# Gathering whole rows, copying them out in slot order and loading them by parts; turning the router's logits on VectorE

## The chip, the cores and the metric

The kernel runs on one core of a Trainium2 chip. The core has a matrix engine (PE), a vector engine (DVE, VectorE), a scalar engine (ACT), a general engine (POOL, GpSimd) and SP, which here only issues DMAs. SP and ACT issue DMAs through hardware queues, POOL through a software queue; all of them end on the same 16 DMA engines. The metric is the device time of one execution in microseconds. Differences are stated against the kernel before.

## What is computed

x has 4 x 1024 tokens of 1024 numbers. The part of the reference that matters here, cut down:

```python
xn = layernorm(x)                       # per token
q, k, v = xn @ Wq.T + bq, xn @ Wk.T + bk, xn @ Wv.T + bv
kv_sum = cumsum((elu(k) + 1) * v, axis=tokens)      # per batch row
s = ((elu(q) + 1) * kv_sum * SCALE) @ Wo.T + bo
logits = xn @ router_w.T                # 8 experts, top 2, at most 256 tokens an expert
h = gelu(buf @ w1.T + b1) @ w2.T + b2   # same weights for every expert
g = silu(sum over the kept experts of probability * h)
out = x + s * g
```

All experts share w1 and w2, so a token needs its h once, and g is zero for a token that no expert kept. So out differs from x in at most 8 x 256 = 2048 tokens.

## The kernel before, in words

Every float32 number goes through PE as a rounded high part and a low part, and each product of two numbers as three matmuls. The work has two stages.

**Token blocks** (to 451 us). The first 2304 tokens go in blocks of 512 (four and a half). A block is normed row by row, its normed rows are stored in HBM (`xnd`), read back by quarters of 256 columns so that 32 x 32 transposes on VectorE turn them (`turned`, L249), and split into `xt`. For each of 8 chunks `kv_block` multiplies by a piece of Wk and one of Wv (L169, 24 matmuls a piece), forms the running sums and stores them in HBM (`kvs`). Side work (norms, transposes, routing, gathers) is laid out in a list of steps by `put`, and `step()` runs the next entry twice per chunk and part. The order on PE, DVE and ACT is written out by hand; on SP and POOL the framework orders the work of this stage, but for instructions marked `in_turn`, which keep program order. The last entry of a step list that concerns this change comes in the last block, which multiplies 512 and 256 tokens side by side and so has 32 steps.

*Router.* `router` (L333 to L355) multiplies each block by the router's weights (`rws`, high and low parts side by side in 16 columns) into `pl` (16 x 512), ACT copies it into `lt` (L344), and one step later `total` turns it on PE: per 128 tokens a matmul of `lt` as weights with `ssum` (L349) that also adds high and low parts; VectorE copies the result into `lg` (L350).

*Lists.* `routing` ranks the experts, finds each token's slot, and scatters token numbers and weights into `lst` in HBM, in slot order, by 18 indirect DMAs (L586). Slots 0 to 2047 are four `Slots` objects of 512. `places` reads the numbers four times over into `raw` and forms `at` = 4 x token + quarter (L617, L623); `load` reads numbers and weights (`it`, L629) and forms `eighth` and `half`.

*Gathers.* `quarters` (4 indirect DMAs for 128 tokens, rows of 1 KB) and `eighths` (4, rows of 512 B) bring rows by `at` and `eighth` straight into the layout that `turned` needs (all at L661). `chosen_items` fetches slots 0 to 1023 into `gx` in the last block, turns them into `work`, and `chosen_sums` forms what the first products need. The first quarters of w1 go into two tiles `raw[0]`, `raw[1]` by loads that are listed at the last block's first step (the framework issues them at 18 and 30 us).

**Products** (from 451 us). Two passes p = 0, 1 over 1024 slots each. A pass has 70 products of 48 matmuls (L1121): a 7-product recursive scheme stands for each 8 quarter products, as `features` (7 products; right operand b from the tokens) and `outputs` (7), for four parts of the hidden layer (w1, w2), then `queries` with Wq and `result` with Wo. Each product takes units a and b (2 + 2 tiles of 1 MB, high and low parts), in three buffers a side. In `features` of all parts but the very first, b is loaded ready-made from HBM (`b<-xtd`, L1091, 2 MB a product; the first part stores it there, L1235); in `result` from `wod`. Quarters of the weights come as `raw` (L834, L1184, 1 MB each). `wprep_items` and `xprep_items` prepare Wo's operands and the next pass's tokens (fetch, turn, split, store in `xtd`, L693) in small buffers (`s4`, eight). The order is written out by `on(n, phase, f)`: step n runs beside product n, in phases load, pre, cast0, evac, low0, add, cast1, mid, low1, post, raw. Here PE, DVE, ACT and SP, and the marked POOL instructions, keep program order.

In this stage `xprep_items` fetches rows for pass 1 by `quarters` (steps 13, 15, 28, 30, into `g`), and `queries` fetches sums by `eighths` (steps 42, 44, 50 and 57 of each pass, into `gk`, turned 2 or 3 steps later). Both are issued by POOL, which doesn't wait for PE and so runs ahead of the steps when buffers are free.

`ht` and `y0` are tiles of 128 x 2048 for one quarter of an operand or result, `raw` are five such.

Of the kernel before, what the change touches and what calls it, by code (L numbers as in the profile page):

```python
# [8 lines left out]
F32 = mybir.dt.float32  # L9
# [28 lines left out]
NC = NT // P  # L38
# [8 lines left out]
def tile_first_tokens(  # L47
# [42 lines left out]


# [15 lines left out]
    acol = cp.tile([P, 1], F32, name="acol")  # L107
    for a in range(NA):
        nc.gpsimd.memset(acol[a * SQ : (a + 1) * SQ], float(a))

    ssum = kp.tile([2 * NE, NE], F32, name="ssum")
    nc.gpsimd.tensor_tensor(
        ssum, ident[: 2 * NE, 0:NE], ident[: 2 * NE, NE : 2 * NE], ALU.add
    )
# [4 lines left out]
    lg = kp.tile([P, NE, NC], F32, name="lg")  # L119

    carry = kp.tile([P, 6 * DC], F32, name="carry")[:, :DC]
# [211 lines left out]
    def router(xt, b, j0, j1):  # L333
# [3 lines left out]
        for k in range(DC):  # L337
            for h in range(2):
                nc.tensor.matmul(  # L339
                    pl[: 2 * NE], rws[:, k], xt[:, h, k, cols],  # L340
                    start=k == 0 and h == 0, stop=k == DC - 1 and h == 1,
                )
        lt = tp.tile([2 * NE, BT], F32, tag="t512", bufs=5, name=f"lt_{b}_{j0}")
        nc.scalar.copy(lt[:, :w], pl[: 2 * NE])  # L344

        def total():
            pr = mmp.tile([P, NJ, NE], F32, tag="mm", name=f"pr_{b}_{j0}")
            for j in range(j1 - j0):
                nc.tensor.matmul(pr[:, j], lt[:, j * P : (j + 1) * P], ssum, start=True, stop=True)  # L349
            nc.vector.tensor_copy(  # L350
                lg[:, :, b * NJ + j0 : b * NJ + j1],
                pr[:, : j1 - j0].rearrange("p j e -> p e j"),
            )
# [247 lines left out]
    class Slots:  # L601


        def __init__(self, s):
# [3 lines left out]
            self.raw = cp.tile([P, NB, 1], I32, name=f"raw_{s}")  # L608
            self.at = cp.tile([P, NB, 1], I32, name=f"at_{s}")
            self.eighth = cp.tile([P, 2, NB], I32, name=f"eighth_{s}")  # L610

        def places(self):

            rows_ap = lst[self.s * BT : (self.s + 1) * BT, :]
            for a in range(NA):
                in_turn(
                    nc.gpsimd.dma_start(  # L617
                        part_of(self.raw, a),
                        rows_ap[:, 0:1].rearrange("(b j) w -> j b w", j=SQ),
                    )  # L620
                )
            in_turn(
                nc.gpsimd.tensor_scalar(self.at, self.raw, float(NA), acol, ALU.mult, ALU.add)  # L623
            )

        def load(self):
# [3 lines left out]
            for h in range(2):  # L630
                nc.gpsimd.tensor_scalar(
                    self.eighth[:, h], self.at[:, :, 0], 2.0, float(h), ALU.mult, ALU.add
                )
                nc.gpsimd.tensor_scalar(
# [6 lines left out]
        def quarters(self, g, src, j):  # L641

            for b in range(NA):
                gather(
                    g[:, b * FQ : (b + 1) * FQ],
                    src.rearrange("n (a f) -> (n a) f", a=NA),
                    self.at[:, j * NA + b],
                )

        def eighths(self, g, src, h, j):  # L650

            for b in range(NA):
                gather(
                    g[:, b * P : (b + 1) * P],
                    src.rearrange("n (a h f) -> (n a h) f", a=NA, h=2),
                    self.eighth[:, h, j * NA + b : j * NA + b + 1],
                )
# [11 lines left out]
    def xprep_items(p, buf):  # L669
# [3 lines left out]
        def item(j):  # L673
            g, v = {}, {}

            def fetch():
                for i in range(2):
                    g[i] = buf(f"g{p}_{j}_{i}")
                    slots[2 * p + i].quarters(g[i], xnd, j)
# [112 lines left out]
    rws = kp.tile([P, DC, 2 * NE], F32R, name="rws")  # L792
# [14 lines left out]

    def chosen_items():


        def item(i, j):
# [10 lines left out]
            slots[i].quarters(g, xnd, j)  # L822
# [809 lines left out]
```

## Time and profile before

| what | us |
| --- | --- |
| median of 17 runs | 2037.32 |
| lowest and highest of the runs | 2020.40, 2047.21 |
| the profiled execution's own time | 2019.86 |
| its span, first to last instruction | 2018.1 |
| DVE busy, ACT busy, POOL busy | 1509.7, 747.0, 418.5 |
| 36 matmuls pr (L349), busy | 4.8 |
| 192 gathers (L661), POOL busy | 151.5 + 45.5 + 33.8 |
| bytes moved by DMA | 400.17 MB, 198 GB/s |

A group in the profile names line, engine, operation, what it writes and reads, the count, busy time, mean ns of one, and the idle time just before with what ended it. A wait line names the engine and line that waited, who released it, the sum, the number of times and the longest. "issue" is a wait for nothing that the profile shows. A timeline line has start, length, engine, line, what and how many. A line of the table by stretches has the stretch, its length, the busy time (and number) of PE, of PE's weight loads, of DVE, ACT and POOL, then the granted clock of PE, the mean busy share of the 16 DMA engines, and GB/s.

### The profile page before, as it was taken

Reading aid. Unit: us, or ns where it says so; the run is one execution under the profiler, and the core shown is the slowest. Engines: PE = TensorE matmul, PEld = TensorE weight load, DVE = VectorE, ACT = ScalarE, POOL = GpSimd, SP = SyncE. Lnnn points to the kernel's source line nnn. Section 1 sums busy time; section 2 is a strip of 40 time slices with the busy share of each in tenths; the row PEclk is TensorE's granted clock in tenths of the full one; section 3 lists DMA queues with packets and bytes.
Section 4 is the critical chain, followed back from the end, with each engine's and each line's share of the span. In section 5 each row is a group of like instructions: output and inputs, shape, how many; then the busy total and the mean of one; then the engine's idle time right before and its main releaser. Section 6 shows DMA issues by size and latency. Waiting matters only on the chain.

```text
span 2018.1 us, 22522 instructions
## 1 busy us (share of the span) xinstructions
PE 1966.5 (97%) x8872; PEld 1621.7 (80%) x8872; DVE 1509.7 (75%) x1422; ACT 747.0 (37%) x876; POOL 418.5 (21%) x403
## 2 busy tenths in 40 slices
PE   8999999999999999999899999999999999999995
PEld 7877877888888788887588888888888888888884
DVE  7868876578897896895597786596586586697794
ACT  3323332225534543542342552342343342342460
POOL 2001103551033124118212016500000000303014
PEclk9999999999999999999899999999999999999998
DMA  8867857638359559547416579715614614715567
GB/s 313 242 194 241 266 143 158 208 121 305 117 200 354 208 195 369 227 147 269 178 48 213 175 260 321 275 42 173 243 42 169 248 42 168 270 45 196 188 205 152
DMA packets 121011, 400.17 MB, mean 198 GB/s; under 512 B 13792, under 2 KB 38368, under 8 KB 99168
## 3 DMA queue, kind: packets, MB, share of 16 engines
q1 hardware_dynamic: 79360, 320.95, 45.6%
q0 software_dynamic: 23104, 61.43, 10.1%
q10 hardware_dynamic: 18432, 16.26, 3.3%
q8 instruction: 72, 1.18, 0.2%
q14 instruction: 43, 0.35, 0.1%
HBM read 317.83 MB, written 88.10 MB: 201 GB/s over the span
## 4 chain that ended last, share of the span: by engine, by line
PE 81%; DVE 9%; DMA 3%; issue 3%; ACT 1%; POOL 1%; SPq 0%; ACTq 0%; DVEq 0%; POOLq 0%
PE ps L1121 63%; PE pk L169 9%; PE pv L169 9%; DMA b<-xtd 2%; DVE a L866 2%; DVE b L866 1%; DVE work L1048 1%; DVE hid L1048 1%; PE pl L339 1%; DVE raw L1045 1%; DVE wo L176 1%; DMA xtd<-o 1%; DVE hid L1045 0%; DMA wr_w<-in_wk 0%; POOL g L661 0%
## 5 line engine op out<-in xcount | busy, mean ns | idle before, releaser
L1121 PE MATMUL ps<-b,a 128*128 128x512 f32 x6720 | 1532.0, 390 | 14.3 <-issue 10.2
L1121 PEld LDWEIGHTS ps<-b,a 128*128 128x128 f32 x6720 | 1262.5, 188 | 283.4 <-issue 21.7
L863 ACT CAST a<-raw 128x1024 fp32r<-128x1024 f32 x140 | 147.1, 1052 | 457.8 <-PE ps L1121 323.0
L866 DVE TENSOR_TENSOR a<-raw,a 128x1024 fp32r<-128x1024 f32 x140 | 170.6, 1221 | 190.8 <-ACT a L863 172.0
L661 POOL DMA_INDIRECT gk<-kvs,eighth x128 | 151.5, 1184 | 605.1 <-DVE kv L249 567.0
L863 ACT CAST a<-hid 128x1024 fp32r<-128x1024 f32 x120 | 125.6, 1050 | 268.7 <-PE ps L1121 225.7
L169 PE MATMUL pk<-xt,ws_w 128*128 128x512 f32 (+1 forms) x792 | 183.1, 386 | 3.4 <-ACT xt L175 2.2
L169 PE MATMUL pv<-xt,ws_w 128*128 128x512 f32 (+1 forms) x792 | 181.8, 385 | 1.3 <-DVE ws_w L176 1.2
L866 DVE TENSOR_TENSOR a<-hid,a 128x1024 fp32r<-128x1024 f32 x120 | 146.2, 1220 | 41.1 <-ACT a L863 41.0
L169 PEld LDWEIGHTS pk<-xt,ws_w 128*128 128x128 f32 x792 | 145.1, 189 | 34.2 <-ACT xt L175 2.7
L169 PEld LDWEIGHTS pv<-xt,ws_w 128*128 128x128 f32 x792 | 145.2, 189 | 31.5 <-DVE ws_w L176 2.6
L1048 DVE TENSOR_TENSOR hid<-ps,hid 128x2048 f32<-128x2048 f32 (+1 forms) x69 | 125.1, 1821 | 57.7 <-PE ps L1121 35.9
L1045 DVE TENSOR_TENSOR raw<-raw,raw 128x2048 f32<-128x2048 f32 x62 | 141.9, 2288 | 0.8
L866 DVE TENSOR_TENSOR b<-raw,b 128x1024 fp32r<-128x1024 f32 x112 | 136.5, 1218 | 0.0
L863 ACT CAST b<-raw 128x1024 fp32r<-128x1024 f32 x112 | 117.3, 1047 | 0.0
L1048 DVE TENSOR_TENSOR work<-ps,work 128x2048 f32<-128x2048 f32 x40 | 91.4, 2286 | 29.2 <-PE ps L1121 29.2
L175 ACT CAST ws_w<-wr_w 128x1024 fp32r<-128x1024 f32 x64 | 66.1, 1049 | 85.8 <-issue 33.4
L1313 ACT ACTIVATE hid<-hid,bs 128x512 f32<-128x512 f32 x104 | 66.7, 713 | 57.4 <-DVE hid L1048 57.4
L176 DVE TENSOR_TENSOR ws_w<-wr_w,ws_w 128x1024 fp32r<-128x1024 f32 x64 | 77.7, 1214 | 10.0 <-ACT ws_w L175 8.7
L375 ACT ACTIVATE kb<-pk,bs 128x512 f32<-128x512 f32 (+1 forms) x40 | 25.9, 646 | 139.1 <-PE pk L169 95.2
L744 POOL DMA_DIRECT2D wod<-wo x28 | 20.2, 723 | 264.1 <-DVE wo L176 244.3
L214 POOL TENSOR_TENSOR r<-ve,mhalf 128x1 f32<-128x1 f32 x18 | 23.0, 1277 | 221.3 <-DVE ve L212 221.3
(183 smaller groups left out, 1292.8 us busy)
## 6 DMA issues: line engine op xcount, KB each, us to landing
b<-xtd SPq DMA_DIRECT2D x126, 1024.0 KB
raw<-in_w SPq DMA_DIRECT2D x64, 1024.0 KB
b<-wod SPq DMA_DIRECT2D x28, 1024.0 KB
wr_w<-in_wk SPq DMA_DIRECT2D x32, 512.0 KB
wr_w<-in_wv SPq DMA_DIRECT2D x32, 512.0 KB
xtd<-b SPq DMA_DIRECT2D x14, 1024.0 KB
wod<-wo POOLq DMA_DIRECT2D x28, 512.0 KB
xtd<-o POOLq DMA_DIRECT2D x28, 512.0 KB
```

The source lines that it names most:

```text
L169: nc.tensor.matmul(ps, ws[:, w, k], mv[:, x, k, c0:c1], start=n == 0, stop=n == len(order) - 1)
L175: nc.scalar.copy(dst[0], src)
L176: nc.vector.tensor_tensor(dst[1], src, dst[0].bitcast(F32), ALU.subtract)
L214: nc.gpsimd.tensor_tensor(r, ve, mhalf, ALU.pow)
L375: nc.scalar.activation(kb, ps, AF.Identity, bias=bcol)
L661: nc.gpsimd.indirect_dma_start(out=dst, out_offset=None, in_=src, in_offset=bass.IndirectOffsetOnAxis(ap=idx, axis=0),)
L863: nc.scalar.copy(self.parts[0], src)
L866: nc.vector.tensor_tensor(self.parts[1], self.src, self.parts[0].bitcast(F32), ALU.subtract)
L1045: nc.vector.tensor_tensor(dst, a, b, ALU.subtract)
L1048: nc.vector.tensor_tensor(dst, a, b, ALU.add)
L1121: nc.tensor.matmul(ps[m] if s["apart"] else ps[:, m], a(h, k, m), b(l, k), start=s["first"] and u == 0 and k == 0 and i == 0, stop=u == 1 ...
L1313: nc.scalar.activation(dst[:, m], src[:, m], AF.Gelu, bias=b1[:, fc : fc + 1])
```

## The change

Router: `rws` is widened to 32 columns, the last 16 zero; `pl` has 32 rows; the ACT copy, the matmuls with `ssum` and the tile `pr` go. `total` has VectorE turn `pl` by 32 x 32 blocks straight out of PSUM (four instructions a block of 512) and add high and low parts.

Gathers: `places`, `quarters` and `eighths` go, and with them `raw` (the list), `at`, `eighth`. For each 128 slots one indirect DMA brings whole rows (4 KB) into half of a tile that is free just then, and a plain DMA on POOL copies them into `xng` (tokens) or `kvg` (sums) in HBM, in slot order. `parts` then loads them by four plain DMAs on SP. Slots 0 to 1023 go through `ht`, `raw[0]` and `raw[1]` in the last block, all listed at its step 10 (six gathers, then copies out and gathers by turns); their loads and turns are listed at new steps, and the w1 quarters for `raw[0]` and `raw[1]` at step 22 in place of 0. Tokens of pass 1 go through `y0` at steps -1 to 7 of pass 0, sums of each pass through `ht` at steps 26 to 34. `fetch` in `queries` stands in the phase raw, that of `xprep_items` in the phase raw one step earlier. `lg` and `carry` get smaller tiles. The core of the diff:

```diff
@@ router
-                    pl[: 2 * NE], rws[:, k], xt[:, h, k, cols],
+                    pl[:SQ], rws[:, k], xt[:, h, k, cols],
...
-        lt = tp.tile([2 * NE, BT], F32, tag="t512", bufs=5, name=f"lt_{b}_{j0}")
-        nc.scalar.copy(lt[:, :w], pl[: 2 * NE])
         def total():
-            pr = mmp.tile([P, NJ, NE], F32, tag="mm", name=f"pr_{b}_{j0}")
-            for j in range(j1 - j0):
-                nc.tensor.matmul(pr[:, j], lt[:, j * P : (j + 1) * P], ssum, start=True, stop=True)
-            nc.vector.tensor_copy(
+            lt = tp.tile([P, BT], F32, tag="t512", bufs=5, name=f"lt_{b}_{j0}")
+            lt = lt[:, : (j1 - j0) * SQ].rearrange("p (j e) -> p j e", e=SQ)
+            for a in range(NA):
+                nc.vector.transpose(
+                    part_of(lt, a),
+                    pl[:SQ].rearrange("i (j a t) -> i a j t", a=NA, t=SQ)[:, a],
+                )
+            nc.vector.tensor_tensor(
...
@@ Slots
+        def gathered(self, dst, src, j, g):
+            r0 = self.s * BT + j * P
+            def rows_in():
+                gather(g, src, self.it[:, j, 0:1])
+            def rows_out():
+                in_turn(nc.gpsimd.dma_start(dst[r0 : r0 + P, :], g))
+            return rows_in, rows_out
+        def parts(self, g, src, j, c0=0, w=FQ):
+            nb = D // w
+            for a, rows_ap in enumerate(by_quarter(src, self.s * BT + j * P, nb, c0, w)):
+                nc.sync.dma_start(part_of(g, a).rearrange("p (b f) -> p b f", b=nb), rows_ap)
@@ last block
-                put([[lambda f=f: turns.append(f())] for f in chosen_items()], at=10 // half)
-                for at in (16, 18, 19, 20, 22, 23, 25, 26):
+                copies = [
+                    slots[j // NJ].gathered(xng, xnd, j % NJ, rows_of((ht, *raw)[j // 2 % 3], j))
+                    for j in range(2 * NJ)
+                ]
+                for k in range(2 * NJ + 6):
+                    if k >= 6:
+                        put([[copies[k - 6][1]]], at=10 // half)
+                    if k < 2 * NJ:
+                        put([[copies[k][0]]], at=10 // half)
+                for at, f in zip((14, 15, 16, 17, 19, 20, 21, 22), chosen_items()):
+                    put([[lambda f=f: turns.append(f())]], at=at // half)
+                for at in (18, 19, 20, 21, 23, 24, 25, 26):
                     put([[lambda: turns.pop(0)()]], at=at // half)
...
-                put([[lambda i=i: left_quarter(raw[i], w1, 0, i)] for i in range(2)])
+                put([[lambda i=i: left_quarter(raw[i], w1, 0, i) for i in range(2)]], at=22 // half)
@@ queries
-            for jj in range(4):
-                slots[2 * p + j].eighths(
-                    g[jj // 2][:, jj % 2 * BT : (jj % 2 + 1) * BT], kvs, i, jj
-                )
+            for half in range(2):
+                slots[2 * p + j].parts(g[half], kvg, 2 * half, i * P, P)
...
-            on(n0 + k, "load", lambda key=key: fetch(*key))
+            on(n0 + k, "raw", lambda key=key: fetch(*key))
@@ passes
+        for j in range(2 * NJ):
+            copies = [(26, slots[2 * p + j // NJ].gathered(kvg, kvs, j % NJ, rows_of(ht, j)))]
+            if p + 1 < NP:
+                sl = slots[2 * p + 2 + j // NJ]
+                copies.append((-1, sl.gathered(xng, xnd, j % NJ, rows_of(y0, j))))
+            for k, (rows_in, rows_out) in copies:
+                on(n0 + k + j, "post", rows_in)
+                on(n0 + k + j + 1, "load", rows_out)
...
-                    on(n0 + k + d, "post" if i else "load", f)
+                    on(n0 + k + d - (i == 0), "post" if i else "raw", f)
```

## The prediction

> **What bounds the kernel now.** I read the page's busy times first, then the timeline of PE, who made PE wait, the table by stretches of one product (10.9 us), and last the groups by line and the queues of POOL and SP.
>
> ```profile
> PE 1966.5 (97%) x8872; PEld 1621.7 (80%) x8872; DVE 1509.7 (75%) x1422; ACT 747.0 (37%) x876; POOL 418.5 (21%) x403
> PE ps L1121 <- issue: 10.2, 14, 1.6
> PE ps L1121 <- DMA b<-xtd: 4.0, 5, 1.1
> ```
>
> PE is busy for 97% of the span, so a change pays only where it takes matmuls off PE or takes away a place where PE runs below its pace. The pace: the chain of waits ends in one piece of 3072 matmuls (64 products of 48) in 696.62 us, 10.88 us a product. Places below it, in PE's timeline:
>
> ```profile
> 957.23 4.95 PE L1121 MATMUL ps<-b,a 128*128 128x512 f32 x20 [0.26 <-issue]
> 962.50 0.72 PE L1121 MATMUL ps<-b,a 128*128 128x512 f32 x2 [0.33 <-issue]
> 963.90 0.39 PE L1121 MATMUL ps<-b,a 128*128 128x512 f32 x1 [0.68 <-issue]
> ...
> 979.44 0.59 PE L1121 MATMUL ps<-b,a 128*128 128x512 f32 x1 [0.81 <-issue]
> 980.84 254.51 PE L1121 MATMUL ps<-b,a 128*128 128x512 f32 x1115 [0.81 <-issue]
> ```
>
> From 957 to 981 us PE issues one or two matmuls each 0.7 or 1.4 us, with nothing in the profile that it waits for ("issue"). From 913.14 to 1235.35 us are 1344 matmuls, 28 products: 322.2 us where 28 x 10.88 = 304.8 are due, so **17.5 us are lost**. There are two smaller places like it in the last token block: 331.01 to 354.24 us takes 23.2 us where two undisturbed weight pieces take 2 x 8.34 (6.6 lost), and 379.26 to 401.50 takes 22.2 where 2 x 8.34 are due (5.6 lost). Together 29.6 us. The busy sums hide part of it, since matmuls also last longer there; the granted clock (the first number after the five busy times) falls once PE idles:
>
> ```profile
> 335.00:350.00 15.00, 11.27 (x50) 8.29 (x49) 5.45 (x10) 2.02 (x2) 8.36 (x8) 0.89 0.90 141
> 385.00:393.00 8.00, 4.85 (x25) 4.18 (x24) 4.17 (x8) 2.21 (x4) 3.15 (x5) 0.83 0.85 258
> 955.00:982.00 27.00, 16.65 (x49) 10.00 (x48) 7.17 (x7) 3.08 (x3) 17.56 (x18) 0.73 0.52 183
> ```
>
> (us, then busy time and count of PE, PEld, DVE, ACT, POOL, then clock, DMA share, GB/s.) What the three have in common is POOL: it issues indirect DMAs back to back, one per 1.25 us, in all of them: the list scatters (320.8 to 346 us), the gathers gx (367 to 419) and 48 gathers gk (904.75 to 977). Against it: g (587 to 616, 751 to 779) and gk from 1050, 1252, 1713 and 1813 us come in such bursts too (that at 1252 of 36), and PE doesn't falter. So the burst may be needed, but it doesn't suffice.
>
> **The change, part by part.**
>
> *Router.* It removes 36 matmuls pr with their weight loads, and the ACT copy. The price is read from the timeline, as weight piece, pr, weight piece: 44.47 to 56.59 us is 12.12 us where two pieces take 10.88, so 1.24; the same at 109.61, 203.68 and 287.43; the half block (228.52 to 240.19) 0.79. Sum 4 x 1.24 + 0.79 = **5.75 us off PE**, which has no other work to put there. pl's weights grow from 16 to 32 columns: its 16 matmuls take 3.73 us, 0.233 each, and a full 128-column one 0.227, so nothing is added. VectorE gains four transposes of 32x128 and an add, and loses a 0.16 us copy. kr's transposes take 702 ns for 512 elements and 436 for 256: 1.04 ns an element and 170 fixed, so 0.30 each, 1.2 + 0.2 per block, some 6 us over five. DVE is at 0.7 to 0.85 here and weights are split three pieces (16 us) ahead of PE; the single PE wait on it was 1.2 us. Cost 0; without that cover 6. The zero columns of rws are one DVE instruction at the start, 0.2 us beside the first weight pieces. One bank of pl is held until the transposes, a step later; of four, two are enough for a chunk: 0.
>
> *Fewer, larger gathers.*
>
> ```profile
> L661 POOL DMA_INDIRECT gk<-kvs,eighth x128 | 151.5, 1184 | 605.1 <-DVE kv L249 567.0 <-issue 36.9 <-DMA gk<-kvs,eighth 0.9
> L661 POOL DMA_INDIRECT g<-xnd,at x32 | 45.5, 1422 | 9.8 <-issue 9.5 <-DMA g<-xnd,at 0.3
> L661 POOL DMA_INDIRECT gx<-xnd,at x32 | 33.8, 1055 | 18.7 <-issue 9.3 <-DVE work L249 9.2 <-DMA out<-in_x 0.3
> ```
>
> 192 gathers become 32 of 4 KB rows, each followed by a plain copy out: POOL goes from 231 us to about 32 x 1.2 + 32 x 0.8 = 64 us, worth nothing in itself (POOL is at 21%). What counts is that the long bursts are gone: six gathers in a row in the last block, then one per product. If bursts make PE falter, 5.6 (gx) and 17.5 (gk) go; the 18 scatters stay, and so do their 6.6. Bounds for this term: -29.6 (all three) to 0 (none); I take **-23.0**, by the bursts that the places lie in. The list loads for slots 0 and 1 shrink from eight of 2 KB to two of 4 KB, on POOL alone.
>
> [...]
>
> *More bytes.* 16.8 MB are now gathered, written and read again: +33.6 MB on 400. All of it has to fit beside PE's loads. The most that a 10.9 us stretch moved is 413 GB/s, 4.4 MB per product. In the first pass, products 29 to 36:
>
> ```profile
> 767.20:778.10 10.90, 10.90 (x50) 9.03 (x49) 4.07 (x5) 3.87 (x3) 7.41 (x8) 1.00 1.00 389
> 788.90:799.80 10.90, 10.90 (x50) 9.03 (x49) 7.19 (x10) 6.49 (x10) 2.58 (x3) 1.00 1.01 398
> 799.80:810.70 10.90, 10.90 (x50) 9.03 (x49) 7.00 (x8) 3.40 (x5) 2.54 (x3) 1.00 1.02 413
> 810.70:821.60 10.90, 10.90 (x50) 9.03 (x49) 8.86 (x9) 4.81 (x8) 2.57 (x3) 1.00 1.02 410
> ```
>
> The queues are full already: per product 2.1 MB of b, 1.05 of raw and 1.5 of xtd<-o are 4.6, and PE waits 0.8 us for b at 825. The copies of sums (steps 26 to 34) add 1.05 MB a product there: 1.05 x 4 = 4.2 MB over, 10 us at 0.41 MB/us. Most falls on POOL's own stores, since its chain of gather, copy, gather has one or two DMAs under way, while SP has several; late xtd<-o stores hold the small buffers that ACT writes (it waited 11.9 us for them before, with 0.8 reaching PE). Bounds 0 and 12; I take **+4**, nearer the row at 825. In the second pass the same steps stand at 290 GB/s (0.80); with 96 more they are just full: **+0.5**. The chosen rows' copies (steps -1 to 7, 451 to 530 us) meet 0.36 to 1.01; there b comes from SBUF and the raw loads have over a product of slack: 0. The gathers that POOL begins at 905 go away, and with them the wait of 0.89 us for b at 913: **-0.9**. (That of 0.27 at 1235 lies beside the accumulating stores, which stay.)
>
> [...]
>
> *Loads moved to SP.* 128 loads at 0.43 us (four xg take 1.74) are 56 us of a queue that waits 653 us for PE in the main part. They stand in SP's order before the next product's b loads, and a part load that had to wait would hold those. What it waits for: the copy out, 8 steps earlier for the sums and over 4 for the rows; and a small buffer: POOL's gathers found theirs at once except where POOL had run ahead of the transposes (waits of 72, 418 and 77 us); SP reaches it four steps after the transposes that free it. Behind them b's first half has 10.9 us until it is needed, and the 3.5 us of issue fit. In the last block the weights' loads are behind them: six gathers from about 360 us, copies out landed by 372 to 390 (an estimate: 1.25 us an issue, some 4 us a landing, like the 3.8 of kvs<-kr in the chain), turns due from 393 us on, and three split pieces (25 us) in hand. raw's w1 quarters move from 18 us to step 22 (about 410), needed at 444. Cost 0; if a load is late, DVE stands and PE after it.
>
> **Sum against the profiled execution:** -5.75 - 23.0 + 4.5 - 0.9 = -25.2; its time of 2019.86 us (span 2018.1) would be 1994.7. It is the fastest of those shown; their median is 2037.32, 17.5 above, and what fills that the profile can't show. I carry the difference over: 2037.3 - 25.2 = **2012 us**.
>
> **Rivals.**
> 1. *The faltering isn't the gathers'* (six bursts without it speak for this): -5.75 + 4.5 - 0.9 = -2.2, 2035 us, within the 0.3% (6 us) that a measurement can tell from no change. 0.13.
> 2. *Slower: the full queues become the bound* at products 29 to 36 of the first pass. PE bears the whole excess (12) and 2 in the second pass, and the faltering stays with the scatters, gathers and copies that remain: 12 + 2 - 5.75 = +8, 2046 us. It decides once the new waits for b and for xtd<-o's buffers pass 6 us more than the faltering that goes. For it: shares of 1.02 there; against: 0.8 us of wait so far. 0.23.
> 3. *Both:* the bursts' loss goes, but the queues take 14: -5.75 - 23.0 - 0.9 + 14 = -15.7, 2022 us. 0.08.
> 4. The forecast, 0.56; its own range is 1990 (all three places go, and some of the 17.5) to 2030.
>
> Faster 0.64, same 0.13, slower 0.23. The range runs from 1990 to 2046.
>
> **What would show it.** Right: no pr; PE's "issue" waits below 5 us and a granted clock of 1.00 at products 43 to 50; DMA at about 434 MB. Wrong: the same 0.7 us steps of PE at gathers or copies, b<-xtd waits above 8 us at products 29 to 36, ACT waiting for xtd<-o more than 20 us, or DVE waiting for gx, g or gk in the turns. If the median of the runs isn't moved by what the profile gains, my carrying over was wrong.

## The result and the profile after

The changed kernel takes 2058.46 us (median of 8 runs, 2054.13 to 2062.83), the kernel before 2035.98 beside it (47 runs, 2017.07 to 2048.35): ratio 1.0118, 95% interval 1.0091 to 1.0145. It is **slower by 22.5 us**, where 2012 was forecast, and lies above the forecast's range (1990 to 2046).

The busy times of the kernel after, and then who made PE wait (us in total, times, longest):

```profile
PE 1975.2 (96%) x8836; PEld 1621.4 (79%) x8836; DVE 1515.0 (74%) x1443; ACT 744.2 (36%) x871; POOL 230.7 (11%) x242
```

```profile
PE pv L163 <- DVE kb L413: 20.4, 1, 20.4
PE pk L163 <- ACT kb L374: 17.7, 1, 17.7
PE ps L1118 <- DMA b<-xtd: 13.9, 9, 3.1
```

The products' wait on "issue" (10.2 us before) is gone, as forecast, and POOL went from 418.5 to 230.7. New are two single waits of 38.1 us in the last token block. The wait for b grew from 4.0 to 13.9. PE's timeline and the table by stretches (columns as for before) show the two stalls and what they do to the clock; the last line is the stretch in which PE of the kernel before did only one or two matmuls at a time:

```profile
371.50 4.75 PE L163 MATMUL pk<-xh,ws_w 128*128 128x256 f32 x24 [17.69 <-ACT kb L374]
396.63 8.50 PE L163 MATMUL pv<-xt,ws_w 128*128 128x512 f32 x24 [20.38 <-DVE kb L413]
```

```profile
350.00:400.00 50.00, 11.93 (x46) 9.96 (x45) 5.98 (x11) 3.57 (x5) 15.79 (x25) 0.60 0.78 261
821.80:843.60 21.80, 19.86 (x88) 16.10 (x87) 16.98 (x18) 7.91 (x11) 6.29 (x8) 1.00 1.02 387
955.00:982.00 27.00, 25.34 (x112) 20.62 (x111) 19.67 (x13) 7.02 (x6) 1.28 (x2) 1.00 0.92 307
```

PE works 11.93 of 50 us from 350 on, at a granted clock of 0.60. Products begin at 492.65 and not at 451.54 us, 41.1 later; the spans of the two profiled executions differ by 39.3 (2057.4 against 2018.1). What stands behind the stalls is in the waits of SP and ACT, and in SP's timeline:

```profile
SPq L636 <- DMA xng<-ht: 53.6, 2, 45.7
ACT kb L374 <- DMA gx<-xng: 40.9, 1, 40.9
ACT ws_w L169 <- DMA gx<-xng: 24.5, 2, 21.3
DVE ws_w L170 <- ACT ws_w L169: 33.8, 11, 21.9
```

```profile
321.65 0.33 SPq L120 DMA_DIRECT2D wr_w<-in_wk  x1
367.78 11.41 SPq L636 DMA_DIRECT2D gx<-xng  x8
379.28 0.38 SPq L120 DMA_DIRECT2D wr_w<-in_wv  x1
386.71 5.38 SPq L636 DMA_DIRECT2D gx<-xng  x8
```

SP stands for 45.7 us at the first part load gx, until the copy out that it reads has landed, and no weight piece is loaded from 321.65 to 379.28 (before, six were, from 327.64 to 374.86). ACT's activation kb doesn't read gx; ACT waits for gx since a copy out<-in_x (L925) stands before it in ACT's order. In the program as built, the copies of ACT and the loads of SP are given the same eight completion semaphores by turns, and this copy waits for the one that the first gx load has to give back. The second stall comes the same way: PE waits for DVE (kb L413), DVE splits a weight piece before that and waits for ACT's half of the split (ws_w L169), and ACT waits behind its next copy for another gx load.

One more thing is in the timeline without a wait, the pace: one weight piece of 24 matmuls starts 5.60 us after the one before it, where it was 5.44, and a product takes 10.93 us in place of 10.89.

### The profile page after: what moved, and what is told of

Read it like the earlier page. It is cut to its first block, busy times and chain, and to the rows that moved or that the text cites. A ratio compares the mean times of both kernels' runs of the same rounds, so it can differ in the third digit from the quotient of the medians.

```text
span 2057.4 us, 22422 instructions
## 1 busy us (share of the span) xinstructions
PE 1975.2 (96%) x8836; PEld 1621.4 (79%) x8836; DVE 1515.0 (74%) x1443; ACT 744.2 (36%) x871; POOL 230.7 (11%) x242
## 2 busy tenths in 40 slices
DMA packets 149171, 433.69 MB, mean 211 GB/s; under 512 B 13280, under 2 KB 62432, under 8 KB 127328
## 4 chain that ended last, share of the span: by engine, by line
PE 82%; DMA 8%; DVE 5%; POOL 2%; issue 1%; ACT 1%; SPq 0%; ACTq 0%; DVEq 0%; POOLq 0%
PE ps L1118 66%; PE pv L163 8%; PE pk L163 8%; DMA b<-xtd 4%; POOL lst L585 1%; PE pl L333 1%; DMA xng<-ht 1%; DMA raw<-in_w 1%; DVE b L849 1%; DVE a L849 1%; DMA gk<-kvg 0%; DVE work L1045 0%; DMA xng<-raw 0%; DMA g<-xng 0%; DMA wr_w<-in_wk 0%
## 5 line engine op out<-in xcount | busy, mean ns | idle before, releaser
L1118 PE MATMUL ps<-b,a 128*128 128x512 f32 x6720 | 1533.9, 390 | 14.0 <-DMA b<-xtd 13.9
L163 PE MATMUL pv<-xt,ws_w 128*128 128x512 f32 (+1 forms) x792 | 187.6, 392 | 20.9 <-DVE kb L413 20.4
L163 PE MATMUL pk<-xt,ws_w 128*128 128x512 f32 (+1 forms) x792 | 188.0, 393 | 3.8 <-ACT xt L169 2.2
L163 PEld LDWEIGHTS pk<-xt,ws_w 128*128 128x128 f32 x792 | 146.2, 190 | 39.3 <-issue 2.9
L169 ACT CAST ws_w<-wr_w 128x1024 fp32r<-128x1024 f32 x64 | 66.1, 1046 | 101.4 <-issue 34.7
L1464 POOL DMA_INDIRECT out<-c,half x8 | 15.3, 1908 | 679.7 <-DVE c L1487 405.5
L376 DVE TENSOR_SCALAR ex<-kb 128x512 f32<-128x512 f32 (+1 forms) x40 | 15.8, 396 | 63.0 <-ACT kb L374 63.0
L640 POOL DMA_INDIRECT ht<-kvs,it x16 | 23.9, 1492 | 245.6 <-DVE a L849 240.9
```

Of the source, the lines that this page charges most:

```text
L163: nc.tensor.matmul(ps, ws[:, w, k], mv[:, x, k, c0:c1], start=n == 0, stop=n == len(order) - 1)
L169: nc.scalar.copy(dst[0], src)
L640: nc.gpsimd.indirect_dma_start(out=dst, out_offset=None, in_=src, in_offset=bass.IndirectOffsetOnAxis(ap=idx, axis=0),)
L1118: nc.tensor.matmul(ps[m] if s["apart"] else ps[:, m], a(h, k, m), b(l, k), start=s["first"] and u == 0 and k == 0 and i == 0, stop=u == 1 ...
```

## Experiments

The kernels of each section but the last ran on one chip, and ratios are to the kernel before on that chip, with 95% intervals. Differences in us are those of the medians; a ratio can differ from the ratio of the medians by some 0.002. The chips are of **two kinds**: on three the kernel before took 1992 to 1998 us, on three 2027 to 2049, much as in the first measurement (2036). Each chip was used in one session only, so what belongs to the chip and what to the session isn't told apart. Below, a chip "falters" where PE slows to single matmuls beside POOL's indirect DMAs, with "issue" as its wait. Kernels on different chips are compared through their ratios, or where the trace shows the place.

### Addresses, and the loads of the last block

The kernel before took 1992.13 us here.

*The kernel before, large tiles moved by 32 bytes:*

```diff
+    cp.tile([P, 8], F32, name="pad")
-    carry = kp.tile([P, 6 * DC], F32, name="carry")[:, :DC]
+    carry = kp.tile([P, 6 * DC + 8], F32, name="carry")[:, :DC]
```

> The kernel before with its large tiles moved by 32 bytes, nothing else, so that xt, work, hid, ht, raw, a2, b2 and y0 start at an address that is 0 mod 64, as they do in the changed kernel, in place of 32 mod 64. Theory A (the changed kernel's slower matmul pace, 0.2333 against 0.2267 us each in the token blocks and 10.93 against 10.89 us a product, comes from where its operands lie): the same two paces appear here, and the time grows by some 10 us in the token blocks and 6 in the products, 2036 to about 2052, ratio 1.008. Rival (the pace comes from the changed kernel's work, such as its wider router weights or its DMAs): paces 0.2267 and 10.89, time 2036, ratio 1.000.

Measured: 2008.63 us, 1.0076 (1.0062 to 1.0090), paces 5.60 and 10.93. Nothing but addresses was changed, so places of tiles cost 16 us (by the ratio 12 to 18). The rule "mod 64" fell later.

*The changed kernel with its tiles back in place* (the same two lines, `4 * DC + 8`):

> The changed kernel with the same 32 bytes put in, so that its large tiles start at 32 mod 64 as in the kernel before. Theory A: pace 0.2267 and 10.89 again, time 2058 less 16, about 2042, ratio 1.003; the two stalls of PE in the last token block (20.4 and 17.7 us) stay. Rival (the work, not the place): 2058, ratio 1.012.

Measured: 2049.78 us, 1.0294 (1.0280 to 1.0308), paces 5.44 and 10.89. The stalls stay, 26.7 and 21.2 us. The absolute numbers of the expectation were for the other kind of chip.

*The changed kernel with the loads gx and of w1's first quarters on POOL:*

```diff
-            slots[i].parts(g, xng, j)
+            slots[i].parts(
+                g, xng, j, issue=lambda *aps: in_turn(nc.gpsimd.dma_start(*aps))
+            )
...
-    [lambda i=i: left_quarter(raw[i], w1, 0, i) for i in range(2)]
+    [lambda i=i: left_quarter(raw[i], w1, 0, i, pool_dma) for i in range(2)]
```

> The changed kernel with two sets of loads of the last token block issued by POOL in place of SP: the 32 part loads gx and the two loads of w1's first quarters, both of which wait for copies out. Theory B (SP stands at the first gx load until its copy out has landed, the weights' loads behind it and, by a completion lane that a waiting gx load holds, ACT's copies of x too; so DVE and ACT stop and PE after them): both stalls go, 38 us and some 5 us of cold clock with them, 2058 to about 2015, ratio 0.990; products begin near 455 us and not at 493. Rival (the added 33.6 MB and the chain of gather, copy, load are themselves too slow, whoever issues): the turns still come late, the products begin 20 us or more late, the time stays above 2040, ratio over 1.002.

Measured: 2017.39 us, 1.0121 (1.0106 to 1.0137); products begin at 454.14, one stall of 11.5 us is left.

*Both:*

> Both mends at once on the changed kernel: the loads on POOL and the 32 bytes. Theories A and B together: 2058 - 43 - 16 = about 2000, ratio 0.982; what then is left against the kernel before is the router (-5.75), the places where PE faltered at gathers (-23.1) and the longer waits for b (+9), by which sum it is 2036 - 20 = 2016, ratio 0.990. If either theory falls, above 2025, ratio over 0.995.

Measured: 2010.40 us, 1.0097 (1.0082 to 1.0113). Theory B holds: the loads that waited in SP's queue, with what stood behind them on SP and ACT, cost 39.4 us (2049.8 to 2010.4). But the kernel is still 18 us above the kernel before, far from the sum. Who made PE wait, here:

```profile
PE ps L1122 <- DMA b<-xtd: 10.3, 5, 3.4
PE pv L164 <- DVE kb L414: 7.8, 1, 7.8
```

The 7.8 are the last block's chain of gather, copy out, load and turn: DVE stands 15.7 us at its first turn, for gx. And nothing is won back by PE's faltering; on this chip the kernel before, by its 1992.13 us, has none to lose.

### Both kernels as they are, and the change in parts

*The changed kernel, unedited:*

> The changed kernel as it is, on the chip on which the four runs before this one put the kernel before at 1992 us, where 2036 had been measured. Theory C (the places where PE falters at POOL's bursts, priced at 23 us, belong to an earlier setting and not to the kernel; here neither kernel has them, so the change has nothing to win back): 2050 (the changed kernel with its tiles moved) + 16 = about 2066, ratio 1.037. Rival (the chip or its setting shifts both kernels alike): ratio 1.012, 2016 us, and the kernel with its tiles moved would then be slower than this one.

Measured: 2060.01 us, ratio 1.0337 (1.0323 to 1.0350) to 1992.22: the changed kernel is as slow here as at first (2058.46), the kernel before is 44 us faster. Theory C's number, 2066, was too high: with the stalls, 10.2 us of the slower pace are left (2060.0 against 2049.8).

*The kernel before, for its profile:*

> The kernel before, for a profile of it beside the others. Theory C: no steps of 0.7 us at 957 to 981 us nor at the two places in the last token block, where the earlier profile lost 29.6 us; span 2018 less some 28 = 1990; the matmul pace 0.2267 us as before. Rival (it is faster here by a higher clock or by faster DMAs, while the faltering stays): the steps are there, and the pace is below 0.2267 us or the waits for b<-xtd are gone.

Measured: 1995.03 us in this one execution, span 1993.2, pace 5.44. Who made PE wait in the products, and the stretch of the gathers gk:

```profile
PE ps L1121 <- DMA b<-xtd: 7.1, 5, 2.5
```

```profile
955.00:982.00 27.00, 27.00 (x121) 22.37 (x120) 19.28 (x12) 12.18 (x15) 8.81 (x9) 1.00 0.62 220
```

121 matmuls where the first profile had 49, clock 1.00 and not 0.73, no wait on "issue" anywhere. The same program with the same burst (POOL issues the 48 gathers gk from 896 to 966 us, mostly one per 1.25 us) doesn't falter on this chip.

*The router's part alone:*

> The kernel before with the router's part of the change alone (the matmuls pr and the ACT copy removed, VectorE turns the logits), its large tiles at the addresses of the kernel before. The prediction's step: 5.75 us off PE, 1992 to about 1986, ratio 0.997. Rival (VectorE's added 6 us delay the splits, or PE waits for the bank of pl): ratio 1.000 or above.

The edit is the router's part of the diff, with `6 * DC + 8` for carry. Measured: 1995.03 us, 1.0022 (1.0011 to 1.0034). The matmuls pr and the gap around them are gone, but the pace is the slow one. Two weight pieces in PE's timeline, of the kernel before (on this chip) and of this one:

```profile
72.67 5.60 PE L169 MATMUL pv<-xt,ws_w 128*128 128x512 f32 x24
78.11 5.60 PE L169 MATMUL pk<-xt,ws_w 128*128 128x512 f32 x24
```

```profile
72.31 5.76 PE L164 MATMUL pv<-xt,ws_w 128*128 128x512 f32 x24
77.91 5.76 PE L164 MATMUL pk<-xt,ws_w 128*128 128x512 f32 x24
```

The starts are 5.44 and 5.60 apart. xt lies as before here; only the weight tiles ws have moved, by 64 bytes, so the rule "mod 64" is wrong. 62 such pieces lose 62 x 0.16 = 9.9 us; the median rose by 2.8, so the router's part itself gives about 7 (5.5 by the ratio; forecast 5.75).

*Slots 0 to 1023 as before* (gathers straight into gx, w1 at the block's first step), the rest of the change, tiles in place:

```diff
-            slots[i].parts(g, xng, j)
+            slots[i].quarters(g, xnd, j)
...
-    put([[lambda i=i: left_quarter(raw[i], w1, 0, i) for i in range(2)]], at=22 // half)
+    put([[lambda i=i: left_quarter(raw[i], w1, 0, i)] for i in range(2)])
```

> The changed kernel with the gathers of slots 0 to 1023 in the last token block as before (32 indirect DMAs straight into gx, w1's first quarters loaded early) and the large tiles at the addresses of the kernel before; the router and the product stage's copies are the changed kernel's. Theory D (once places and addresses are mended, what remains of the loss, 18 us against the kernel before, is the last block's chain of gather, copy out, load and turn, some 12, and the full queues at products 29 to 36, some 6): no stall of PE in the last block, waits for b<-xtd of 10 to 13 us, 1992 - 5.75 + 8 = about 1994, ratio 1.001. Rival (the 33 MB cost more than the waits show, by slower matmuls or slower evacuation): ratio over 1.005, as with the loads on POOL and the tiles moved (1.0097).

Measured: 1996.62 us, 1.0021 (1.0011 to 1.0030). No stall in the last block; waits for b 13.0 us. So the last block's chain costs 13.8 us even with its loads on POOL (2010.4 to 1996.6), and the product stage about +10 (1996.6 - 1992.2 + 5.75). That is by the medians: the two profiled executions, this one 2.7 us below its median and the kernel before's 2.8 above, have product stages of 1558.4 and 1554.5 us.

### What of the addresses, and which bytes

This chip is of the other kind: the kernel before took 2042.77 us.

*The router's part, ws at 96 mod 128:* `6 * DC + 24` for carry.

> The router's part alone once more, with the weight tiles ws 64 bytes further on, so that they start at 96 mod 128 as in the kernel before and not at 32 as in the first try (which took 5.60 us for 24 matmuls of the token blocks although xt lay as before). Theory A2 (the address of the weight tile mod 128 sets the pace: 5.44 us where it is 96, 5.60 where it is 32; the router itself gives its 5.75): 5.44 us, 1992 - 5.75 = about 1986, ratio 0.997. Rival (the router's part itself slows the pace, by its 32-column weights or its zeros): 5.60 us, ratio 1.002 as in the first try.

Measured: 2051.99 us, 1.0028 (0.9998 to 1.0058), token blocks at 5.58. Theory A2 fell.

*The kernel before, xt and its like at 0, ws at 96:* the pad and `6 * DC + 24`.

> The kernel before with xt, work, hid, ht, raw, a2, b2 and y0 at 0 mod 128 and the weight tiles ws at 96 as before: the other half of the first move, which had both. Theory A2 (the weight tile decides): token blocks keep 5.44 us for 24 matmuls; products, whose tile a2 (one of the three that serve as weights) now lies at 0, take 10.93 us and not 10.89; 1992 + 6 = about 1998, ratio 1.003. Rival (the right operand xt decides as well, or both must agree): 5.60 us in the token blocks, 2008, ratio 1.008.

Measured: 2063.29 us, 1.0098 (1.0059 to 1.0137), 5.62 us. The rival holds: xt counts as well. By the programs as built, fast kernels have both tiles at 224 mod 256; the slow ones had the two at different places.

*The sums too as before* (128 gathers straight into gk, no kvg); router and copies of pass 1's tokens stay:

```diff
-            for half in range(2):
-                slots[2 * p + j].parts(g[half], kvg, 2 * half, i * P, P)
+            for jj in range(4):
+                slots[2 * p + j].eighths(
+                    g[jj // 2][:, jj % 2 * BT : (jj % 2 + 1) * BT], kvs, i, jj
+                )
```

> As the kernel with gx as before (1996.6 us, ratio 1.002), with the sums too gathered as before (128 indirect DMAs straight into gk, no kvg, no copies through ht): of the change remain the router and the copies of pass 1's tokens. Theory D2 (the product stage's +10 us is the sums' copies at steps 26 to 34, where the queues were full already; prediction's step 'more bytes', which gave them 4): waits for b<-xtd at 740 to 870 us fall to the 3 to 7 of the kernel before, 1988, ratio 0.998. Rival (it is the token copies at steps -1 to 8 or the loads on SP): waits and time stay, 1996, ratio 1.002.

Measured: 2036.95 us, 0.9951 (0.9925 to 0.9976), waits for b 2.7 us. Theory D2 holds: against the kernel before this one gains 5.8 us (by the ratio 10, 5 to 15), about the router's part, and the one with the sums copied lost 4.4; so the sums' copies cost 10 us by the medians. By the two ratios, which come from chips of different kinds, it is 14 (9 to 19).

*The changed kernel, tiles in place, without ACT's copies of x* (the rows of out behind the first 2304 tokens stay unwritten): `range(nt, nt, P)` for `range(nt, NT, P)` at L926.

> The changed kernel with its tiles at the old addresses (2050 us, stalls of PE of 26.7 behind ACT and 21.2 behind DVE), without ACT's fourteen copies of x into out (the rows of out behind the first 2304 tokens are left out). Theory B in its second half (ACT is held by these copies, which wait for a completion lane that a gx load holds): ACT's stall goes, DVE's stays, 2050 - 27 = about 2023, ratio 1.015. Rival (PE would wait in any case, since the weights behind SP's waiting load come late for ACT too): the wait takes another name, the stalls still sum to 40 or more, 2045, ratio 1.027.

Measured: 2016.87 us, 0.9853 (0.9811 to 0.9895). Both stalls together are one of 8.3 us, behind ACT, so more went than the theory said. But the edit changed two things. The framework now also orders SP otherwise, with four more weight loads ahead of the first gx load, and SP waits for copies out of ht for 15.7 us in place of 54.0 with the copies of x:

```profile
SPq L637 <- DMA xng<-ht: 15.7, 2, 9.3
```

```profile
356.70 0.33 SPq L121 DMA_DIRECT2D wr_w<-in_wk  x1
366.35 1.76 SPq L637 DMA_DIRECT2D gx<-xng  x4
```

So what ACT's wait cost and what SP's late weight loads cost isn't separated, and the rival isn't out. This kernel is 26 us faster than the kernel before, which falters on this chip: PE waits on "issue" only at the list scatters here (334 to 344 us, 4.5 us), while the two kernels above it, which kept the gathers gx and gk, waited 26 and 29 us, most of it beside gx and gk (377 to 400 and 949 to 1006).

### PE alone, and the mends

*A kernel of matmuls alone* (the changed part is a new body; 48 matmuls for each pair of places, then phases beside POOL and SP):

> Not the reference's work (all of it is left out; out receives rows of x): PE alone, 48 matmuls of the token blocks' form for each of 64 pairs of places, the weight tile moved by 0 to 224 bytes in steps of 32 and the right operand likewise, then 66 us each of matmuls beside nothing, beside 48 gathers of 512-byte rows back to back on POOL, beside loads of 1 MB on SP, beside loads and such gathers, beside loads and 48 plain DMAs on POOL, beside loads and 24 gathers spaced by a memset. Theory A3 (fast where both operands start at 224 mod 256, which the fast kernels have in common and the slow ones do not: 224 and 32, 0 and 96, 192 and 160, 224 and 96 all took 5.58 to 5.62 us): 0.2267 us a matmul in few of the 64 pairs, 0.233 in the rest, by a rule that can be read from the table. Rival (it isn't the operands' place, but something else that moved with them): one pace in all 64. Of the faltering, on a chip that has it: theory (gathers back to back, as against plain DMAs or spaced ones): steps with no releaser in the two phases with gathers in a burst and not in the others; rival (any DMAs of POOL, or the full queues): in the phase of plain DMAs or of loads alone too. On a chip without it: none anywhere.

Measured on a chip where the kernel before took 2049.12 us. Start to start of 48 matmuls, us; rows are the bytes by which the weight tile is moved, columns those of the right operand (unmoved, both start at the same place mod 256, at 128):

```
        x0   x32   x64   x96  x128  x160  x192  x224
w0    10.88 11.20 11.00 11.21 11.20 11.24 11.19 11.19
w32   11.19 10.88 11.21 11.00 11.21 11.20 11.24 11.19
w64   11.19 11.20 10.91 11.20 11.00 11.21 11.20 11.23
w96   11.24 11.21 11.19 10.91 11.20 11.00 11.21 11.20
w128  11.20 11.24 11.19 11.19 10.89 11.20 11.00 11.21
w160  11.21 11.15 11.24 11.21 11.20 10.90 11.20 11.00
w192  10.98 11.21 11.20 11.25 11.20 11.20 10.90 11.20
w224  11.20 10.99 11.21 11.20 11.24 11.19 11.19 10.90
```

Fast is the diagonal, **both starts equal mod 256**: 10.9; with the right operand 64 further on 11.0; all else 11.15 to 11.25. It is not one tile's address but the difference. That gives every kernel here (weight tile, right operand, us for half as many): before 224 and 224, 5.44; changed 160 and 192, 5.60; router alone 32 and 224, 5.60; then 96 and 224, 5.58 (5.60 by the table); last 96 and 0, 5.62 (11.24 in the table).

The phases, in the table by stretches (240 matmuls, 54.4 us undisturbed): gathers in a burst, loads alone, loads and burst, loads and plain DMAs, loads and spaced gathers.

```profile
824.90:922.80 97.90, 65.11 (x241) 48.42 (x240) 0.16 (x1) 0.00 (x0) 45.66 (x49) 0.76 0.11 32
933.70:988.10 54.40, 54.40 (x242) 45.05 (x241) 0.29 (x3) 0.00 (x0) 0.00 (x0) 1.00 0.97 376
999.00:1099.00 100.00, 63.04 (x241) 48.09 (x240) 0.34 (x3) 0.00 (x0) 45.50 (x49) 0.76 0.70 263
1109.90:1164.30 54.40, 54.40 (x241) 45.05 (x240) 0.36 (x3) 0.00 (x0) 25.73 (x49) 1.00 0.98 361
1175.20:1229.60 54.40, 54.40 (x242) 45.05 (x241) 0.47 (x3) 0.00 (x0) 46.36 (x49) 1.00 1.02 388
```

48 gathers back to back cost PE 43.5 us (97.9 - 54.4) at a DMA share of 0.11, and 45.7 at 0.70 (46.7 when repeated). Full queues (0.97 to 1.02), plain DMAs and 24 gathers with a memset of 1 us after each cost it nothing.

*The copies of x beside products 76 to 102* in place of the last block, tiles in place, nothing left out:

```diff
+    for k, r0 in enumerate(range(nt, NT, P)):
+        on(
+            76 + 2 * k, "post",
+            lambda r0=r0: nc.scalar.dma_start(out[r0 : r0 + P, :], x[r0 : r0 + P, :]),
+        )
```

> The changed kernel with its tiles at the old places and ACT's fourteen copies of x into out issued beside products 76 to 102, so that nothing is left out. Theory B, second half, as the run without these copies had it (stalls of PE 8.3 us in place of 48): 2050 - 37 = about 2013 where PE doesn't falter, ratio 1.010; on a chip where the kernel before falters (2043) the same 2016, ratio 0.987. Rival (the run without copies gained because 16 MB of traffic were gone, and they cost the same elsewhere): above 2035.

Measured: 2016.92 us, 0.9852 (0.9814 to 0.9890), stall 5.5 us. So the gain doesn't come from leaving the copies out. SP's order is again the one with four more weight loads first.

*All mends at once* (this, the loads on POOL, tiles in place):

> As that, and with the loads gx and of w1's first quarters on POOL: all that the last block's order cost is mended, the change's work is whole. Expected: no stall of PE in the last block above 8 us; 2003 where PE doesn't falter (1992 - 5.75 for the router + 10 for the sums' copies + 6 for the last block's late turns), ratio 1.005; 2008 on a chip where the kernel before takes 2043, ratio 0.983. Rival (POOL's order is as bad as SP's): no gain over the one with the loads on SP.

Measured: 2006.14 us, **0.9791** (0.9752 to 0.9830): 43 us faster than the kernel before on this kind of chip, stall 3.2 us. On the other kind it wasn't run; its nearest relative there has 1.0097, and with 4.6 us less of stall (7.8 to 3.2) I estimate 1.007, since there is no faltering to win back.

*Number or rate of the gathers*, the kernel of matmuls with six phases of 480 (108.8 us undisturbed, by their starts):

> Not the reference's work (all of it is left out; out receives rows of x): PE alone, 480 matmuls (108.9 us undisturbed) in each of six phases beside POOL, no other DMAs: 48 gathers of 512-byte rows back to back (60 us); 48 of them, each followed by a memset of 1 us; 48 in groups of six, each group followed by six memsets; 12 back to back; 32 gathers of whole 4 KB rows back to back; 48 back to back again. In the sweep 48 back to back cost 43.5 us and 24 spaced ones nothing, but the loss began with the twentieth gather, so number and spacing were not yet apart. Theory (the rate decides: PE runs dry once POOL has issued some twenty with no pause): the two bursts lose some 43 us, spaced, groups of six and twelve nothing, whole rows some 15 to 25 (from the twentieth on). Rival (the number decides): the 48 spaced and grouped ones lose as much as the burst. On a chip without faltering: 108.9 us in all six.

The chip was of the kind that doesn't falter: all six phases took 108.8 us.

> The same kernel once more, since the chip of the run before showed no faltering at all (108.9 us in all six phases; the kernel before took 1998 us on it). On a chip where the kernel before takes some 2040: by the theory that the rate decides, the two bursts lose some 43 us and the 48 spaced and grouped gathers nothing; by the rival that the number decides, these lose as much. On a chip where it takes some 1992: 108.9 us in all six again.

Measured on a chip where the kernel before took 2027.33: the bursts lost 42.2 and 43.6 us, 32 whole rows back to back 25.2, the 48 spaced ones, the 48 in sixes and the 12 nothing. **The rate decides** (in runs that are long enough; 12 back to back cost nothing). PE's timeline, in the first burst and beside the spaced and grouped gathers:

```profile
46.82 21.70 PE L78 MATMUL burstm<-xr,wr 128*128 128x512 f32 x95
...
78.60 0.58 PE L78 MATMUL burstm<-xr,wr 128*128 128x512 f32 x1 [2.21 <-issue]
81.39 0.59 PE L78 MATMUL burstm<-xr,wr 128*128 128x512 f32 x1 [2.21 <-issue]
...
111.50 86.52 PE L78 MATMUL burstm<-xr,wr 128*128 128x512 f32 x366 [2.21 <-issue]
...
208.73 108.96 PE L78 MATMUL spacedm<-xr,wr 128*128 128x512 f32 x480
...
328.41 108.96 PE L78 MATMUL sixesm<-xr,wr 128*128 128x512 f32 x480
```

PE runs 95 matmuls, then falls to about one in 2.8 us, and is back at full pace 4 us after POOL's last gather (107.5). The DMA queues from 68 to 112 us, first on the chip that doesn't falter, then on the one that does:

```profile
q0 software_dynamic: 1056, 2.16, 19.4%
q8 instruction: 2, 0.03, 0.3%
q14 instruction: 1, 0.01, 0.0%
```

```profile
q0 software_dynamic: 1056, 2.16, 17.1%
q14 instruction: 1, 0.01, 0.0%
```

On the first, two packets of q8, a queue of the kind "instruction" in the profile, come while POOL gathers (at 71.2 and 100.4 us); on the second none comes from 46 to 114.7. Whether this is a cause of the slow steps or only a sign of them isn't shown. The two packets are 29.2 us apart, 129 matmuls by the pace there (108.8 us for 480), and in the first measurement the kernel before has 72 packets of q8 for 8872 matmuls, one for 123; so, by my estimate from these, a PE that anything else slows leaves fewer packets, too. What the six slow phases of the two kernels of matmuls have in common is when the slow steps begin: 20.3 to 22.7 us after the phase's first matmul. In the first burst of each kernel the first gather starts 0.79 us after that matmul, and the next ones follow at one per 1.25 us; by these numbers it is at about the 16th to 18th gather. What slows PE, and why only on some chips, the runs don't show.

## Why the prediction was wrong, step by step

The ladder, on chips that don't falter, by medians:

| step | us |
| --- | --- |
| kernel before | 1992.2 |
| router (part of the change, forecast -5.75) | -5.75 as forecast; by the run about -7 |
| sums' copies (forecast +4.5 with both passes) | +10 by what is left, to 1996.6 |
| last block: gather, copy, load, turn (forecast 0) | +13.8, to 2010.4 |
| its loads on SP, and ACT's copies behind them (forecast 0) | +39.4, to 2049.8 |
| tiles at unequal places (not forecast; 16 in the kernel before, here partly hidden by the stalls) | +10.2, to 2060.0 |

On chips that falter, the kernel before starts at 2036 and the changed one ends at 2058: of its 68 us of loss, 44 are hidden by what the kernel before loses to its own gathers.

- **"Loads moved to SP": this step failed.** It gave "Cost 0", with "the weights' loads are behind them", "copies out landed by 372 to 390" and three split pieces (25 us) in hand. The landing was about right for the first (its gx load went at 367.78). Wrong was when SP would stand there. The step took the loads at their listed steps, 14 to 22; but on SP the framework orders this stage, and it put the first gx load directly behind the weight load of 321.65, so that SP stood for 45.7 us and not for a few. And the step named SP's queue alone: ACT, whose copies of x share completion semaphores with SP's loads, was not in it, and both of PE's stalls hang on ACT's waits for gx (40.9 and 21.3 us). What SP's late weight loads would have cost without ACT's waits stays open: both kernels without the copies in the last block (stalls of 8.3 and 5.5 us in place of 48) also have SP's loads in another order. "If a load is late, DVE stands and PE after it" is what came, with ACT between. The turns themselves, 13.8 us, are in the same step: three DMAs one after the other (gather, copy out, load) where there was one, and turns that were due before these had landed.
- **"Fewer, larger gathers", -23.0: right in its mechanism, too small.** PE does falter by POOL's bursts of gathers, and the change takes gx and gk away, as the places of the waits and the phases show. The size came from nearly the fastest execution of the kernel before; by its medians on the two kinds of chip it is 44 us (2036 against 1992), nearly all of which the change wins, as far as the mended kernels show it (2006.1 where PE falters, 2010.4 for the nearest one where it doesn't). "The burst may be needed, but it doesn't suffice" was right, too. Five of the six bursts that spoke against it have 16 gathers, and in the kernels of matmuls PE goes slow only at about the 16th to 18th (in the kernel before, in the first measurement, at the 15th of gx, 386.4 us, and the 32nd of gk, 957.0); the sixth, of 36, cost PE 1.0 to 4.8 us of "issue" in the three kernels that kept it on the chip of "What of the addresses, and which bytes". And it takes the chip or its session. Rival 1 is out.
- **Carrying over the 17.5 us between profile and median: wrong.** The step held that the profile can't show what fills them. The ranges say that it is faltering, which differs from run to run (the kernel before ranges over 31 us where it falters, over 9 where it doesn't); the changed kernel has little of it (4.9 us of "issue" at the list scatters), and its median (2058.46) is that of its profiled execution (2059.25).
- **"More bytes", +4: mechanism right, mis-sized.** It measured about 10, near the bound of 12; the b<-xtd waits went from 4.0 to 13.9 us, 9.6 of them at 804 to 879 us, where the sign of being wrong (above 8) was set and where rival 2 had them. But that rival's place and price, 2046 by full queues, was not what made the kernel slower: the last block was.
- **Router, -5.75: right.** What it gave was eaten by the pace. The price of removing and resizing small tiles (acol, raw, at, eighth, carry, lg) was taken as nothing; they moved xt against ws.
- The -0.9 for b at 913 us can't be told apart in waits for b that grew.
- The four signs of being right all came: no pr, no "issue" wait in the products, a clock of 1.00 there, and 433.69 MB. None of them looks at the last block, where the loss was.
- That DVE and the bank of pl would not be late, and that the tokens' copies beside products 1 to 9 cost nothing, held: the kernel with these alone gained 5.8 us (by the ratio 10, 5 to 15).

## What to carry to other kernels

Before a DMA that waits for another DMA is given to a queue, read what stands behind it in that queue's final order, and whose completion semaphores it holds; here a load that was priced at nothing stopped two engines (39.4 us). Keep a matmul's weight tile and right operand at the same address mod 256 (10.9 us for 48 matmuls here, 11.0 to 11.25 elsewhere), and look at start-to-start times after any change of small tiles. Break runs of more than a dozen indirect DMAs by a pause (after every one, or every six: nothing lost here, against 42 to 47 us for 48 back to back on chips that falter), and measure on more than one chip before a gain is put down to an edit.

## What the runs showed of the hardware

- 48 matmuls of 512 columns take 10.9 us when both operands start equal mod 256, 11.0 with the right one 64 bytes further, else 11.2 (2.9% more), in the kernel of matmuls with 64 pairs of places; 24 of the token blocks take 5.44 with both at 224 and 5.58 to 5.62 at unequal places. So the pace hangs on the two addresses together; what makes it isn't shown. Why a product of the changed kernel takes 10.93 and not 10.89 us is open: its weight and right tiles agree mod 256 in each of the three buffers (one at 192, two at 224).
- On three of six chips PE slows to about one matmul in 2.8 us while POOL issues indirect DMAs back to back. In the two kernels of matmuls on such chips this begins at about the 16th to 18th; 42 to 47 us are lost per 48, none for 12 or when a memset of 1 us stands between. On the other three PE has no wait on "issue" in the kernel before, the router's part alone, the changed kernel with both mends and the second kernel of matmuls.
- PE's granted clock falls with it: 0.76 from 824.9 to 922.8 us, the first burst of the first kernel of matmuls, against 1.00 in the phase with loads alone; and 0.60 from 350 to 400 us of the changed kernel, around the stalls of the last block.
